# Graph layer and expert layer: first edge runs read at fixed places, adjacency columns in six groups, a third of the weighting on GpSimd, x weighed before it is normalised

## The chip, the core and the metric

The kernel runs on one core of one Trainium2 chip. The metric is device time in microseconds (us), start to end, of one execution. The engines named below are TensorE (PE, with PEld for its weight loads), VectorE (DVE), ScalarE (ACT), GpSimd (POOL) and SyncE (SP, which here only issues DMAs).

## The reference, cut to what matters

```python
# x: 2048 x 256; src, dst: 67584 edges, sorted by dst; edge_weight: one per edge
# node_vec1: 2048 x 1; 8 experts, W1 256 x 1024, W2 1024 x 256
def gnn(xn, values, indices, bias):
    row, col = indices
    return segment_sum(values[:, None] * xn[col], row, 2048) + bias
def ffn(xt, ...):                        # top 2 of 8 experts per token
    top_p, top_idx = top_k(softmax(xt @ Wr + br), 2)
    weights = top_p / top_p.sum(-1)
    xe = layernorm(xt) * ln_g[e] + ln_b[e]
    y = gelu(xe @ W1[e] + b1[e]) @ W2[e] + b2[e]
    return sum over the two experts of weights * y
x = x + gnn(layernorm(x), edge_weight, stack([src, dst]), node_vec1)
x = x + ffn(layernorm(x))
```

All of it is float32. The change touches only the graph layer, and what is prepared beside it.

## The kernel before, in words

**The graph layer as dense products.** The sparse matrix is turned into a dense one of 2048 x 2048, column block by column block, and then multiplied by the normalised x. There are 16 column blocks (`NB`) of 128 nodes. Since `dst` is sorted, the edges of two neighbouring nodes lie in one window of 128 edges. A quarter-like unit `q` (8 of them) covers 128 such pairs of nodes, one on each partition.

- `find_blocks`, `get_run`, `count_before` and `get_win` find where each pair's window starts. The first edge of each of 128 stretches (`first_i`) is spread over the partitions with a small matmul, compared with the nodes' numbers (`less`), and gives a stretch; an indirect DMA from the POOL queue fetches that stretch (`run`, 528 edges), ACT counts the edges before the pair (`sign`), and three more indirect DMAs fetch the window's sources, destinations and weights (`win_s`, `win_d`, `win_w`).
- `keys_of` makes two keys of each edge (source modulo 128; node of the pair and source block), `turn_keys` turns them and the weights with TensorE, and `next_part` splits a weight into three bf16 parts (`w`, three wide) that add up to the float32 value.
- `make_hots(n)` works on a half block, 32 pairs of nodes, of which there are 32. Three DVE instructions (L293, L296, L300): `hl` is one where an edge has a given low key, `eq` one where it has a given high key, and `hr` is `eq` times the three weight parts. All three read two bf16 tensors in SBUF.
- `make_cols(n)` multiplies them: 96 small TensorE matmuls (L320), three parts for each pair; ACT copies the result out (`ar`, L323), a DMA writes it to device memory (`ad`), and after every second half block another DMA reads the whole column block back as `ac` (L327).
- `dense(g, b)` multiplies group `g` of column blocks (`CB` = 4 blocks a group) by `xn_sb`, for two row blocks: 8 products, each of two float32 matmul records (L334). `add` adds the two results into `acc` on DVE (L339).

**The order.** It is written out by hand (`manual_schedule`), engine by engine in the order of the program. A loop over the 32 half blocks makes the hots of `n + 1`, adds what the last half block multiplied, makes the columns of `n`, and from half block 9 on multiplies an older group. Keys and parts of later units, the layer norm's statistics (`block_stats`), the normalising of x (`xn_sb`, L439), its turning and the router's part of it (L446, L456) lie at fixed half blocks. Ten of the 16 blocks' statistics are taken before the loop, six after its first half block. After the loop the last group (blocks 12 to 15) is multiplied beside the router's work (`square`, `roots`, `scales`, `logits`, `best`, `count`, `choose`): 64 products, in eight steps `p` of 8. Then the experts run, the same in both kernels.

**Queues.** SP issues `ad` and `ac` in program order. POOL issues the indirect DMAs in program order; in the loop they come in sets of four (three windows, one run).

Of the kernel before, what the change touches and what calls it, by code (L numbers as in the profile page):

```python
# [22 lines left out]
P = 128  # L23
# [4 lines left out]
def kernel(  # L28
# [45 lines left out]
    CB = 4  # L74
# [19 lines left out]
    first_i = xpool.tile([P, 1], I32, name="first_i")  # L94
    nc.sync.dma_start(first_i, dst.rearrange("(p j) -> p j", p=P)[:, 0:1])

# [3 lines left out]
    for q in range(4):  # L100
        s = slice(q * NB // 4, (q + 1) * NB // 4)
        (nc.sync, nc.scalar)[q % 2].dma_start(acc[:, s, :D], xv[:, s, :])
    nv_rows = small.tile([NB, P], F32, name="nv_rows", bufs=1)
    nc.sync.dma_start(nv_rows, node_vec1.rearrange("(b p) o -> b (p o)", p=P))
    b1_rows = small.tile([NE * KH, P], F32, name="b1_rows", bufs=1)
    nc.sync.dma_start(b1_rows, b1.rearrange("e (c p) -> (e c) p", p=P))
    g_rows = small.tile([NE * KD, P], F32, name="g_rows", bufs=1)
    nc.sync.dma_start(g_rows, ln_g.rearrange("e (k p) -> (e k) p", p=P))
    be_rows = small.tile([NE * KD, P], F32, name="be_rows", bufs=1)
    nc.sync.dma_start(be_rows, ln_b.rearrange("e (k p) -> (e k) p", p=P))  # L110
    wr_sb = consts.tile([P, KD, NE], F32, name="wr_sb")
    nc.scalar.dma_start(wr_sb, Wr.rearrange("(k p) e -> p k e", p=P))
    br_sb = consts.tile([P, NE], F32, name="br_sb")
    nc.scalar.dma_start(br_sb, bass.AP(tensor=br.tensor, offset=br.offset, ap=[[0, P], [1, NE]]))


    ident = consts.tile([P, P], F32, name="ident")
    make_identity(nc, ident)
    jp = consts.tile([P, P], I32, name="jp")
# [3 lines left out]
    ones = consts.tile([P, P], F32, name="ones")  # L123
    nc.vector.memset(ones, 1.0)
    ones_b = consts.tile([P, P], BF16, name="ones_b")
    nc.vector.memset(ones_b, 1.0)
    iota_p = consts.tile([P, P], F32, name="iota_p")
    nc.gpsimd.iota(iota_p, pattern=[[1, P]], base=0, channel_multiplier=0,
                   allow_small_or_imprecise_dtypes=True)
    eps_sb = consts.tile([P, 1], F32, name="eps_sb")  # L130
    nc.vector.memset(eps_sb, EPS)
# [23 lines left out]

    iota_b = consts.tile([P, P], BF16, name="iota_b")
    nc.vector.tensor_copy(iota_b, iota_p)
    iota_h = consts.tile([P, P], F16, name="iota_h")
    nc.vector.tensor_copy(iota_h, iota_p)
    col0 = consts.tile([P, GQ], F32, name="col0")  # L160
    nc.gpsimd.iota(col0, pattern=[[GC * P, GQ]], base=0, channel_multiplier=GC,
                   allow_small_or_imprecise_dtypes=True)
    col16 = consts.tile([P, GQ], F32, name="col16")
    nc.vector.tensor_scalar(col16, col0, -float(NB), None, op0=OP.mult)
    colm = consts.tile([P, GQ], F32, name="colm")
    nc.vector.tensor_scalar(colm, col0, -1.0, -0.5, op0=OP.mult, op1=OP.add)
    colp = consts.tile([P, GQ], F32, name="colp")
    nc.vector.tensor_scalar(colp, col0, 1.0, -0.5, op0=OP.mult, op1=OP.add)
    c15 = consts.tile([P, 1], F32, name="c15")
    nc.vector.memset(c15, 1.5)  # L170

    cols_1 = gnn.enter_context(tc.tile_pool(name="cols_1", bufs=CB))
    ps_s = gnn.enter_context(tc.tile_pool(name="ps_s", bufs=2, space=PSUM))
    edges = gnn.enter_context(ExitStack())
    cols_0 = edges.enter_context(tc.tile_pool(name="cols_0", bufs=CB))
    pool = lambda name, bufs, **k: edges.enter_context(tc.tile_pool(name=name, bufs=bufs, **k))
    find = pool("find", 1)
    one_d = lambda t: t.rearrange("(e o) -> e o", o=1)  # L180
    wins = [None] * GQ
    runs = [None] * GQ
# [3 lines left out]
    mid = find.tile([P, GQ], F32, name="mid")  # L186
# [3 lines left out]
    def find_blocks(pf, q0, q1):  # L190
        less = find.tile([P, GQ, P], F32, name="less")
        l = less[:, q0:q1, :]
        nc.vector.tensor_tensor(l, pf[:, None, :].to_broadcast([P, q1 - q0, P]),
                                col0[:, q0:q1, None].to_broadcast([P, q1 - q0, P]), OP.is_lt)
        nc.vector.tensor_reduce(blk[:, q0:q1], l, AX.X, OP.add)
        nc.vector.tensor_scalar(blk[:, q0:q1], blk[:, q0:q1], -1.0, 0.0, op0=OP.add, op1=OP.max)
        nc.vector.tensor_copy(blk_i[:, q0:q1], blk[:, q0:q1])
        nc.vector.tensor_scalar(mid[:, q0:q1], blk[:, q0:q1], float(EJ), EJ / 2, op0=OP.mult,
                                op1=OP.add)
# [10 lines left out]
    def count_before(q):  # L210
        sign = find.tile([P, EJ], BF16, name="sign")
        nc.scalar.activation(sign, runs[q], AF.Sign, bias=colp[:, q:q + 1], scale=-1.0,
                             accum_out=at[:, q:q + 1])
# [21 lines left out]

# [4 lines left out]
    rowsp = pool("rowsp", 3)  # L240
# [7 lines left out]
    def keys_of(q):  # L248


        s_i, d_i, _ = wins[q]
        cl = prep.tile([P, P], F32, name="cl")
        nc.scalar.activation(cl, d_i, AF.Identity, bias=col16[:, q:q + 1], scale=float(NB))
# [3 lines left out]
        nc.vector.scalar_tensor_tensor(f[:, 0, :], b_i, -float(P), s_i, op0=OP.mult, op1=OP.add)  # L257
        nc.vector.tensor_tensor(f[:, 1, :], cl, b_i, OP.add)
        return f

    def turn_keys(q, f):


        pk = ps_k.tile([P, 3, P], F32, name="pk")
        for i in range(2):
            nc.tensor.transpose(pk[:, i, :], f[:, i, :], ident)  # L266
        nc.tensor.transpose(pk[:, 2, :], wins[q][2], ident)
        w2 = keys.tile([P, P, 3, 2], BF16, name="w2")
        nc.scalar.copy(w2[:, :, 0, :], pk[:, 2, :, None].to_broadcast([P, P, 2]))
        k2 = keys.tile([P, 2, P, 2], BF16, name="k2")  # L270
        for i in range(2):
            nc.scalar.copy(k2[:, i], pk[:, i, :, None].to_broadcast([P, P, 2]))
        parts[q] = (k2, w2, pk[:, 2, :])
# [5 lines left out]
    def next_part(q, i):  # L279

        k2, w2, rest = parts[q]
        r = prep.tile([P, P], F32, name=f"r{i}")
        nc.vector.tensor_tensor(r, rest, w2[:, :, i - 1, 0], OP.subtract)  # L283
        nc.scalar.copy(w2[:, :, i, :], r[:, :, None].to_broadcast([P, P, 2]))
        parts[q] = (k2, w2, r)

    def make_hots(n):


        k2, w2, _ = parts[n // 4]  # L290
        g = n % 4
        hl = hotl.tile([P, GH, P], BF16, name="hl")
        nc.vector.tensor_tensor(hl.rearrange("p g (n t) -> p g n t", t=2),  # L293
                                two(k2[:, 0], g, P), pair(P), OP.is_equal)
        eq = hotr.tile([P, GH, RK], BF16, name="eq")
        nc.vector.tensor_tensor(eq.rearrange("p g (n t) -> p g n t", t=2),  # L296
                                two(k2[:, 1], g, RK), pair(RK), OP.is_equal)
        hr = hotr.tile([P, GH, 3, RK], BF16, name="hr")
# [3 lines left out]
            eq[:, :, None, :].to_broadcast([P, GH, 3, RK]),  # L302
            w[:, :, None, :].to_broadcast([P, GH * 3, RK // 2, 2]), OP.mult)
        return hl, hr

    def make_cols(n, hl, hr):


        cb, h = n // 2, n % 2
        if h == 0:  # L310
            ads[cb] = dram.tile([P, NB, P], F32, name="ad", bufs=CB)
        ad_v = ads[cb].rearrange("(m j) b r -> (j b) m r", m=GB // QP)
        ar = rowsp.tile([P, GH // QP, P], F32, name="ar")
        for m0 in range(0, GH // QP, 4):
            pa = ps_a.tile([P, 4, P], F32, name="pa")
# [28 lines left out]
    with tc.manual_schedule(engines=ALL):  # L344
# [29 lines left out]
        for n in range(NH):  # L374
# [16 lines left out]
            for p in late:  # L391
                add(*p)
# [709 lines left out]
```

## Time and profile before

| What | Value |
|---|---|
| median of 14 runs | 525.72 us (521.97 to 533.76) |
| profiled execution, its own time | 523.11 us |
| its span | 521.3 us |
| busy in the span: PE, DVE, ACT, POOL | 450.0, 282.4, 190.4, 156.0 us |
| busy from 27.69 to 207.03 us (the loop from the second `hl` to the last `hr`): PE, DVE, ACT, POOL | 151.84, 167.00, 74.19, 44.84 us of 179.34 |
| busy from 207.03 to 257.23 us (last group, router): PE, DVE | 48.44, 23.73 us of 50.20 |
| busy from 257.23 us to the end (experts): PE, DVE | 246.63, 74.26 us of 264.07 |

Busy time is what the instructions of an engine cover in a stretch; an engine that covers nearly all of a stretch sets its length there, and one that covers little of it waits or has nothing to do. The three stretches have different limits, so the shares over the whole span say little about any of them.

### The profile page before, as it was taken

The page shows a single profiled execution, that of the slowest core. Times are in us where ns is not written, and L with a number is a line of the kernel's source. Part 1 is how long each engine was busy: PE and PEld are TensorE (multiplying, and loading weights), DVE is VectorE, ACT ScalarE, POOL GpSimd, SP SyncE. Part 2 cuts the span into 40 slices and gives each one's busy share as a digit, 9 for nine tenths or more (in the row PEclk, how much of TensorE's full clock was granted, in tenths as well). Part 3 has the DMA queues.
Part 4 walks back from the last instruction along what each step waited for, and adds up shares of the span by engine and source line. Part 5 has one row for each costly group of instructions (what it writes and reads, how often), then busy time and mean ns, then how long its engine had stood idle before and what let it go on. Part 6 is the DMA issues. An engine that isn't in the chain of part 4 may idle for free. (4 is left out here: it accounts for less than half of the span.)

```text
span 521.3 us, 12093 instructions
## 1 busy us (share of the span) xinstructions
PE 450.0 (86%) x4996; PEld 386.0 (74%) x4996; DVE 282.4 (54%) x594; ACT 190.4 (37%) x438; POOL 156.0 (30%) x127
## 2 busy tenths in 40 slices
PE   0144887999999889899999999999999999997991
PEld 0043786787777678788887888888888888886881
DVE  5698999998999997227848222243323222210011
ACT  1424886432242411037483332323233333322220
POOL 3504044360512000000142444544344334422321
PEclk9986799999999999999999999999999999999997
DMA  6215776776657567795513997799998767748421
GB/s 208 72 42 145 222 233 216 221 238 210 180 176 212 166 175 240 251 347 174 175 53 81 291 334 206 215 353 367 349 335 275 198 175 191 207 108 285 122 105 37
DMA packets 87604, 106.75 MB, mean 205 GB/s; under 512 B 8640, under 2 KB 77360, under 8 KB 85424
## 3 DMA queue, kind: packets, MB, share of 16 engines
q1 hardware_dynamic: 78032, 90.73, 54.4%
q0 software_dynamic: 8032, 14.04, 11.6%
q10 hardware_dynamic: 1472, 1.06, 0.7%
q8 instruction: 44, 0.72, 0.6%
q14 instruction: 24, 0.20, 0.1%
HBM read 79.78 MB, written 28.14 MB: 207 GB/s over the span
## 5 line engine op out<-in xcount | busy, mean ns | idle before, releaser
L919 PE MATMUL ph<-xeT,w 128*128 128x256 f32 (+1 forms) x576 | 123.9, 372 | 5.5 <-PEq L1059 3.9
L334 PE MATMUL py<-xn_sb,ac 128*128 128x264 f32 x512 | 120.9, 391 | 5.0 <-DMA ac<-ad 3.3
L933 PE MATMUL py<-w,hT 128*128 128x256 f32 x544 | 120.6, 379 | 0.0
L919 PEld LDWEIGHTS ph<-xeT,w 128*128 128x128 f32 x576 | 105.1, 192 | 20.3 <-issue 5.3
L921 ACT ACTIVATE hT<-ph,ec 128x256 f32<-128x256 f32 (+1 forms) x144 | 65.9, 461 | 136.9 <-PE ph L919 83.3
L334 PEld LDWEIGHTS py<-xn_sb,ac 128*128 128x128 f32 x512 | 95.0, 190 | 24.3 <-DMA ac<-ad 4.1
L933 PEld LDWEIGHTS py<-w,hT 128*128 128x128 f32 x544 | 102.0, 190 | 13.2
L941 POOL DMA_INDIRECT y_d<-ys,to_i x30 | 48.9, 1631 | 110.1 <-DVE ys L936 90.3
L320 PE MATMUL pa<-hl,hr 128*32 128x128 bf16 x3072 | 55.8, 234 | 20.8 <-DVE hr L300 17.1
L293 DVE TENSOR_TENSOR hl<-k,iota_b 128x4096 bf16<-128x4096 bf16 x32 | 73.1, 2284 | 0.9 <-PE pa L320 0.9
L320 PEld LDWEIGHTS <-hr 128*32 128x32 bf16 x3072 | 49.1, 104 | 29.5 <-DVE hr L300 18.7
L851 POOL DMA_INDIRECT xs<-xr_d,to_i x40 | 41.9, 1047 | 66.9 <-DVE r L617 40.2
L300 DVE TENSOR_TENSOR hr<-eq,w 128x3072 bf16<-128x3072 bf16 x32 | 56.3, 1758 | 2.0 <-DVE eq L296 0.5
L936 DVE SCALAR_TENSOR_TENSOR ys<-py,wt,b2w 128x256 f32<-128x256 f32 x34 | 16.3, 483 | 75.0 <-PE py L933 60.4
L893 DVE TENSOR_SCALAR xeT<-px,ec 128x256 f32<-128x256 f32 (+1 forms) x38 | 18.4, 526 | 63.3 <-PE px L884 56.8
L323 ACT COPY ar<-pa 128x512 f32<-128x512 f32 x64 | 35.6, 585 | 34.1 <-PE pa L320 33.3
L222 POOL DMA_INDIRECT win_s<-in_src,at_i x8 | 11.7, 1456 | 92.4 <-DVE r L283 87.8
L339 DVE TENSOR_TENSOR acc<-acc,py 128x528 f32<-128x528 f32 x32 | 22.1, 698 | 21.5 <-PE py L334 21.5
L908 ACT ACTIVATE b2w<-b,wt 128x256 f32<-128x256 f32 x36 | 16.3, 500 | 27.8 <-DVE wt L906 22.5
L266 PE MATMUL pk<-ident,f 128*128 128x128 f32 x16 | 4.5, 333 | 21.1 <-DVE f L257 16.5
L296 DVE TENSOR_TENSOR eq<-k,iota_b 128x1024 bf16<-128x1024 bf16 x32 | 21.9, 684 | 0.0
L266 PEld LDWEIGHTS pk<-ident,f 128*128 128x128 f32 x16 | 2.3, 153 | 23.3 <-issue 13.3
(193 smaller groups left out, 308.9 us busy)
## 6 DMA issues: line engine op xcount, KB each, us to landing
w<-in_L_ffn_W SPq DMA_DIRECT2D x44, 1024.0 KB, 9.3
ad<-ar SPq DMA_DIRECT2D x32, 512.0 KB, 5.1
ac<-ad SPq DMA_DIRECT2D x16, 1024.0 KB, 5.8
b<-in_L_ffn_b SPq DMA_DIRECT2D x22, 128.0 KB, 9.9
out<-y_d SPq DMA_DIRECT2D x4, 512.0 KB, 6.3
xr_d<-rec SPq DMA_DIRECT2D x1, 1300.0 KB, 6.6
y_d<-acc SPq DMA_DIRECT2D x1, 1280.0 KB, 5.9
acc<-in_x ACTq DMA_DIRECT2D x2, 512.0 KB, 5.5
```

The source lines that it names most:

```text
L293: nc.vector.tensor_tensor(hl.rearrange("p g (n t) -> p g n t", t=2), two(k2[:, 0], g, P), pair(P), OP.is_equal)
L296: nc.vector.tensor_tensor(eq.rearrange("p g (n t) -> p g n t", t=2), two(k2[:, 1], g, RK), pair(RK), OP.is_equal)
L300: nc.vector.tensor_tensor(hr.rearrange("p g i (n t) -> p (g i) n t", t=2), eq[:, :, None, :].to_broadcast([P, GH, 3, RK]), w[:, :, None, : ...
L320: nc.tensor.matmul(pa[j * RK:(j + 1) * RK, m, :], hr[:, g, i, :], hl[:, g, :], start=(i == 0), stop=(i == 2), tile_position=(0, j * RK))
L323: nc.scalar.copy(ar[:, m0:m0 + 4, :], pa)
L334: nc.tensor.matmul(pa[:, i, :DX], acs[g * CB + c][:, b + i, :], xn_sb[:, g * CB + c, :], start=(c == 0), stop=(c == CB - 1))
L339: nc.vector.tensor_add(acc[:, b:b + 2, :], acc[:, b:b + 2, :], pa[:, :, :DX])
L851: nc.gpsimd.indirect_dma_start(out=(sets[s.set][0] if into is None else into)[:, t, :], out_offset=None, in_=(xr_d if rows is None else ro ...
L919: nc.tensor.matmul(ph, w1[:, k, c * P:(c + 1) * P], xeT[:, k, :], start=(k == 0), stop=(k == KD - 1))
L921: nc.scalar.activation(hT[:, c, :s.n * P], ph, AF.Gelu, bias=ec[:, c:c + 1], scale=1.0)
L933: nc.tensor.matmul(py, hT[:, c, t * P:(t + 1) * P], w2[:, c, :], start=(c == 0), stop=(c == KH - 1))
L941: st = nc.gpsimd.indirect_dma_start(out=y_d[:, :], out_offset=bass.IndirectOffsetOnAxis(ap=tos[s.to][:, t:t + 1], axis=0), in_=ys, in_offs ...
```

## The change

In words, by place in the code:

- **Start.** The stretch in which the first unit's windows are looked for (`run_0`, 656 edges a partition) is read by three plain DMAs from fixed places, issued from SP and ACT ahead of x. The first unit needs no search; `find_blocks` is called once for the other seven, with a bf16 `less`, after the first windows are asked for. An activation of the square root stands first on ACT. x is loaded behind `run_0`.
- **Keys.** `keys_of` and `turn_keys` are cut into `low_key`, `high_key`, `turn_key`, `turn_weights` and `count_own`, which are placed one by one.
- **Hots.** `hr` has two weight parts instead of three on DVE. The third part has its own tile (`w3`), and GpSimd multiplies it by `eq` into `hr3`, a tensor_tensor of 128 x 1024 bf16.
- **Columns.** Results are copied out and stored in two halves of 64 partitions' worth of nodes, and each half block is read back by itself (`load_cols`), one half block later.
- **Groups.** Column blocks are multiplied in groups of 2, 2, 3, 3, 3 and 3. In each half block up to `QUOTA` = 8 products are issued, as soon as a group has been complete for `LAG` half blocks. The results are added at the start of the next half block (`do_adds`). The first group's adds also add `node_vec1` (`add_first`), which ACT added before.
- **x.** x is turned and multiplied by the router's weights before it is normalised; a DVE multiplication scales the product (`weighed_x`). Statistics are taken two blocks a half block inside the loop, and normalising goes four blocks at a time.
- Some pools have more buffers: `rowsp` 5 instead of 3, `cols_0` 8 instead of 4, one more `tos`.

```diff
-    CB = 4
+    STEP = E // NG
+    BACK = 4 * STEP
+    RUN_0 = 2 * BACK + P
+    GROUPS = (2, 2, 3, 3, 3, 3)
+    CB0 = 8
+    QUOTA = 8
+    LAG = 3
...
+    nc.scalar.activation(warm_s, eps_sb, AF.Sqrt)
+    run_0 = find.tile([P, RUN_0], I32, name="run_0")
+    nc.sync.dma_start(run_0[16:, :], part(dst, 16 * STEP - BACK, STEP, P - 16, RUN_0))
+    nc.scalar.dma_start(run_0[:nf, :], part(dst, 0, 0, nf, RUN_0))
+    nc.scalar.dma_start(run_0[nf:16, :], part(dst, 0, STEP, 16 - nf, RUN_0))
...
+    def turn_key(q, f, i):
+        nc.tensor.transpose(pk[:, i, :], f[:, i, :], ident)
+        nc.scalar.copy(k2[:, i], pk[:, i, :, None].to_broadcast([P, P, 2]))
...
     def next_part(q, i):
-        nc.scalar.copy(w2[:, :, i, :], r[:, :, None].to_broadcast([P, P, 2]))
+        nc.scalar.copy(w2[:, :, 1, :] if i == 1 else w3, r[:, :, None].to_broadcast([P, P, 2]))
...
-        hr = hotr.tile([P, GH, 3, RK], BF16, name="hr")
+        hr = hotr.tile([P, GH, 2, RK], BF16, name="hr")
         nc.vector.tensor_tensor(
             hr.rearrange("p g i (n t) -> p (g i) n t", t=2),
-            eq[:, :, None, :].to_broadcast([P, GH, 3, RK]),
-            w[:, :, None, :].to_broadcast([P, GH * 3, RK // 2, 2]), OP.mult)
+            eq[:, :, None, :].to_broadcast([P, GH, 2, RK]),
+            w[:, :, None, :].to_broadcast([P, GH * 2, RK // 2, 2]), OP.mult)
+        hr3 = hotr.tile([P, GH, RK], BF16, name="hr3")
+        nc.gpsimd.tensor_tensor(hr3.rearrange("p g (n t) -> p g n t", t=2),
+                                eq.rearrange("p g (n t) -> p g n t", t=2),
+                                two(w3, g, RK), OP.mult)
...
+    def load_cols(n):
+        cb, h = n // 2, n % 2
+        nc.sync.dma_start(acs[cb][h * GH * GC:(h + 1) * GH * GC], ads.pop(n))
...
+    def add_first(b, pa):
+        for i in range(2):
+            nc.vector.scalar_tensor_tensor(acc[:, b + i, :D], pa[:, i, :D], nv_c[:, b + i:b + i + 1],
+                                           acc[:, b + i, :D], op0=OP.add, op1=OP.add)
+        nc.vector.tensor_add(acc[:, b:b + 2, D:], acc[:, b:b + 2, D:], pa[:, :, D:DX])
...
+        count_before(0)
+        get_win(0)
...
+        find_blocks(pf, 1, GQ)
+        get_run(1)
+        get_run(2)
+        get_run(3)
+        xTs = {0: turn_x(0)}
+        b_i, f = low_key(0)
+        turn_key(0, f, 0)
+        block_stats(bn, mv, acc, range(0, 1))
+        high_key(0, b_i, f)
+        turn_key(0, f, 1)
+        hl = make_hl(0)
+        turn_weights(0)
+        next_part(0, 1)
+        eq = make_eq(0)
+        next_part(0, 2)
+        hots = {0: (hl, *make_hr(0, eq))}
...
         for n in range(NH):
+            do_adds()
             if n + 1 < NH:
                 hots[n + 1] = make_hots(n + 1)
...
+            for i in range(2):
+                make_cols(n, i, *hots[n])
+            if n > 0:
+                load_cols(n - 1)
+            while ready < last_g and 2 * group_of[ready][-1] + 1 + LAG - (not jobs) <= n:
+                for b in range(0, NB, 2):
+                    box = []
+                    jobs += [(ready, b + j, c, box) for j in range(2) for c in group_of[ready]]
+                ready += 1
+            more_dense(QUOTA)
...
+            if n < 8:
+                b0 = 4 * (n // 2)
+                if n < 7:
+                    block_stats(bn, mv, acc, range(2 * n + 2, 2 * n + 4))
+                if n % 2 == 0:
+                    weigh_x(b0, xTs.pop(b0))
+                else:
+                    scale_x(b0, 4)
+                    weighed_x(b0, 4)
+                    if b0 + 4 < NB:
+                        xTs[b0 + 4] = turn_x(b0 + 4)
...
-        for p in late:
-            add(*p)
+        load_cols(NH - 1)
+        while jobs:
+            more_dense(2 * max(GROUPS))
+            do_adds()
+        do_adds()
```

In the changed program DVE's order in a half block of the loop is: the adds of the last half block, `hl`, `eq`, `hr`, then that half block's key or part work and statistics. POOL's order is `hr3` of each half block, and every four half blocks the set of three or four indirect DMAs ahead of the next `hr3`.

## The prediction

> **What bounds the kernel now.** I read the page's groups first, then busy time by stretch, then who waits for whom, then DVE and POOL in order of time. The experts' stretch (257 us to the end) is untouched, so all lies in the first 257 us. The costliest groups there, from the page (columns: busy us, mean ns of one, idle time before it and its cause):
>
> ```profile
> L320 PE MATMUL pa<-hl,hr 128*32 128x128 bf16 x3072 | 55.8, 234 | 20.8 <-DVE hr L300 17.1
> L293 DVE TENSOR_TENSOR hl<-k,iota_b 128x4096 bf16<-128x4096 bf16 x32 | 73.1, 2284 | 0.9 <-PE pa L320 0.9
> L300 DVE TENSOR_TENSOR hr<-eq,w 128x3072 bf16<-128x3072 bf16 x32 | 56.3, 1758 | 2.0 <-DVE eq L296 0.5
> L339 DVE TENSOR_TENSOR acc<-acc,py 128x528 f32<-128x528 f32 x32 | 22.1, 698 | 21.5 <-PE py L334 21.5
> ```
>
> The columns' matmuls wait for DVE's `hr`; `hl` hardly ever waits. The stretches (columns: PE, PEld, DVE, ACT, POOL busy) say the same of the loop:
>
> ```profile
> 27.69:207.03 179.34, 151.84 (x3451) 127.76 (x3452) 167.00 (x181) 74.19 (x171) 44.84 (x22) 0.94 0.64 192
> ```
>
> DVE covers 167.0 of 179.3 us, PE 151.8. So DVE sets the loop, and PE would at about 20 us less. Before the loop a chain of transfers sets the time, after it a chain of small DVE and ACT work.
>
> The row that matters most for what is added is how POOL stands to DVE. In order of time (start, duration), DVE and then POOL:
>
> ```profile
> 85.22 2.28 DVE L293 TENSOR_TENSOR hl<-k,iota_b 128x4096 bf16<-128x4096 bf16 x1
> 87.42 0.68 DVE L296 TENSOR_TENSOR eq<-k,iota_b 128x1024 bf16<-128x1024 bf16 x1
> 88.14 1.76 DVE L300 TENSOR_TENSOR hr<-eq,w 128x3072 bf16<-128x3072 bf16 x1
> ```
> ```profile
> 41.76 0.94 POOL L222 DMA_INDIRECT win_s<-in_src,at_i  x1 [18.73 <-DVE r L283]
> ...
> 85.33 2.99 POOL L222 DMA_INDIRECT win_s<-in_src,at_i  x1 [13.15 <-DVE r L283]
> 88.62 2.09 POOL L222 DMA_INDIRECT win_d<-in_dst,at_i  x1 [0.30 <-issue]
> ```
>
> An indirect DMA takes POOL 0.94 us when DVE is free of the three hot instructions. Started under one, it ends 0.82 us after that instruction's end: 88.32 against 87.50 (`hl`), 90.71 against 89.90 (`hr`). POOL, which has indices to read from SBUF, is held for as long as a DVE instruction reads two SBUF tensors, and gets in when it ends. Under the adds (PSUM and SBUF) it is not held: 0.95 us at 107.03.
>
> **The change part by part.** The sum is made against the profiled execution, 523.1 us (span 521.3). That is 2.6 us under the median of the runs, 525.7, and I add 2.6 at the end.
>
> *Start.* Rows before:
>
> ```profile
> 10.55 1.28 ACT L212 ACT_TABLE_LOAD   x1 [10.55 <-DMA run<-in_dst,blk_i]
> 11.85 0.73 ACT L212 ACTIVATE sign<-run,colp 128x528 bf16<-128x528 int32 x1
> ...
> 13.33 0.95 POOL L222 DMA_INDIRECT win_s<-in_src,at_i  x1 [4.27 <-DVE at_i L218]
> ```
>
> `run_0` heads the queues at 0.76 us. A tiny load landed in 2.05 us (`first_i`), a run of nearly this size beside x in 5.0 (5.53 to 10.55). I take 4.0, so 4.8 us. `sign` over 656 instead of 528 elements takes 0.91, its accumulator 0.19, and the two DVE steps and the way to POOL 0.65 as now: the windows are asked for at 6.5 us, not 13.33: -6.8. The table is loaded earlier by the square root (the trace shows `sign` running after that table without a new load). From there to `hl(0)`, at 22.61, it was 9.3 us, with a second unit's keys and two weight parts ahead of it. With only the two keys ahead it is `f` (17.94), turned (0.47) and copied (0.38), 18.9 on the old clock, 5.6 us after the windows: -3.7. From `hl(0)` to `hl(1)` the parts, `eq` and the statistics now lie between: 5.8 instead of 5.1, and 0.8 of POOL's hold: +1.5. Start: **-9.0** (ends: -5, if `run_0` needs the 5.0 us and the windows queue behind x; -11).
>
> *DVE in the loop, POOL left aside.* 1024 elements cost 0.537 us ((1.758 - 0.684) / 2), so `hr` saves 0.537 x 31 = -16.6. Adds: 20 lie in the stretch now; six groups make 48 of them, some 38 in the stretch. 30 plain ones, +10 x 0.65 = +6.5. Eight `add_first`, each two of the 0.483 us kind (L936) and a small one, 1.1: +8.8. Statistics of 14 blocks instead of 6, 0.57 each: +4.6. Four small scalings: +1.5. Together +4.8. DVE's waits for ACT's key copies (2.4 and 1.5 us) and for `cols` (1.6) should go, -5. So **0**: what the smaller `hr` saves is eaten by adds and statistics.
>
> *GpSimd's part.* `hr3` waits for `eq`, is held by `hr`, gets in when `hr` ends, and reads two SBUF tensors. No row shows DVE waiting for POOL. If POOL's reading excludes DVE's as DVE's excludes POOL's, DVE's next two-input instruction waits T, the time of `hr3`. T's bounds come from POOL's rows:
>
> ```profile
> L837 POOL IOTA place<- 128x256 f32 x1 | 0.3, 345 | 2.5 <-DVEq L495 2.5
> masks.py:199 POOL TENSOR_SCALAR_AFFINE_SELECT ident<-ident 128x128 f32<-128x128 f32 x1 | 0.3, 283 | 0.0
> ...
> L128 POOL IOTA iota_p<- 128x128 f32 x1 | 0.2, 233 | 0.0
> ```
>
> Iota, which only writes: 0.875 ns an element, 0.12 us fixed: 1.0 us for 1024, the low end. The select, which reads one and writes one: 1.27 ns, 1.4 us. Two reads at that rate: 2.7 us, the high end. I take 1.4, the only row with a read. Of the 31 stretches from `hr` to the next `hl`, 14 begin with key work or the second part, which read two SBUF tensors, and wait all of T. 17 begin with adds or statistics, which do not, and hide 0.8 on average. 14 x 1.4 + 17 x 0.6 = **+30** (1.0: +18; 2.7: +70; no exclusion: 0).
>
> The Trainium skill's page "SBUF — State Buffer" ("Who interferes with whom") says that a DVE instruction with two SBUF inputs and a GpSimd instruction that reads SBUF exclude each other for the whole instruction, whichever came first. The trace shows it in one direction; the rule speaks against this change, and without the other direction the sum would lose the 30. "GPSIMD Engine Reference" (section 3.1) gives 4497 ns for a two-input add of 2048; half of that is an estimate of 2.25 us, and 14 x 2.25 + 17 x 1.45 = 56 would make the time 569.
>
> *PE.* All 256 products stay. 16 move into the loop, +7.6 us (32 records of 0.239 apart) on 151.8: hidden while DVE takes 179 or more; without that cover PE's floor is 159.5.
>
> *Columns' DMAs.* The same bytes in 64 stores and 32 loads on SP. A load now queues behind the next half block's stores, but a group is used three half blocks after its last column (over 15 us), against 5.1 us for a store and 5.8 for a load: 0. Of the last group it is used 16 products and the branch later (7.4 + 1.4), the same as now: 0 to +1.
>
> *After the loop.* Rows now:
>
> ```profile
> 235.87 0.70 DVE L339 TENSOR_TENSOR acc<-acc,py 128x528 f32<-128x528 f32 x1 [2.86 <-PE py L334]
> ...
> 244.63 2.89 DVE L738 TENSOR_TENSOR chosen<-pos,place 128x1280 f32<-128x1280 f32 x2
> ...
> 247.48 8.80 PE L746 MATMUL px<-chosen,rec 128*128 128x256 f32 x40
> ```
>
> The last group is 48 products, 22.9 us instead of 30.6. But `chosen` ends 11.65 us after the fifth step's add, and that is DVE and ACT work that stays. Up to that add PE does five steps of 6 products instead of 8, 14.4 instead of 18.2. **-3.8**; then the small work is late, and PE waits some 3 us for it. ACT's 16 additions of `node_vec1` (0.5 each) cost nothing now and gain nothing.
>
> Sum: 523.1 - 9.0 + 0 + 30 - 3.8 = 540.3, and 2.6: **543 us**.
>
> **The rivals.**
> - *A: POOL does not hold DVE; faster.* `hr3` lies beside DVE, and only start and end count: 523.1 - 12.8 + 2.6 = 513 (507 if the loop also loses DVE's other waits). For it: in no row is DVE late after a POOL read, `hl` takes 2.28 us each time. Against: those reads are only indices. It decides where DVE loses under 12.8 us, 0.4 us a half block.
> - *B: POOL's queue.* Even so, the sets of indirect DMAs stand ahead of `hr3`. Six sets took 7.4, 8.6, 10.7, 8.8, 8.2 and 6.0 us, mean 8.3, while POOL has some 4.4 us free between two `hr3`: 3.9 x 6 = 23 us of PE waiting, of which DVE, a half block ahead, wins back about half: 513 + 12 = 525, up to 536.
> - *C: columns late.* If SP's split stores and loads take twice the time to land, PE waits at each of five groups some 2 to 3 us, on top of A: 525.
>
> **How the numbers follow.** My case 0.55, A 0.27, B 0.14, C 0.04. My case alone runs from 531 (T of 1.0) to 567 (T of 2.2). The range has to reach A: 507 to 566; above lie T beyond 2.2, below a PE-bound loop. A measurement tells about 0.5% (2.6 us) from no change. Faster: A and a little of B and C, 0.29. Within 0.5%: half of B and C, 0.08. Slower: 0.63.
>
> **What would show it.** Right: a gap of about T ahead of the instruction after `hr` on DVE, `hl` spaced 6.5 to 7 us apart instead of 5.2 to 6, PE waiting in the loop for `hr3`, the first `hl` at about 12 us, `chosen` some 26 us after the last group's first product. Wrong, if DVE's spacing is that of its own durations (A), or PE waits for `hr3` only once in four half blocks, behind the sets (B), or on `ac` (C).

## The result, and the profile after

The changed kernel takes 574.5 us (median of 10 runs, 573.2 to 575.0), the kernel before 525.9 us beside it (47 runs, 520.5 to 534.6): ratio 1.0936, 95% interval 1.0908 to 1.0965. The forecast was 543, with a range of 507 to 566. It had the sign right and the size wrong: the time lies above the range. The experiments were run on three chips, on which the kernel before took 530.9 to 534.5 us in the median. Their ratios leave out runs in a slower state, so they are not the quotients of the medians. Differences in microseconds between two experiments are taken between their own medians; where two experiments ran on different chips, the ratios are the safer comparison.

The profiled execution took 573.3 us, with a span of 571.5, against 523.1 and 521.3 before. The page's groups that answer to those shown of before (busy us, mean ns of one, idle time before it and its cause):

```profile
L336 POOL TENSOR_TENSOR hr<-eq,w 128x1024 bf16<-128x1024 bf16 x32 | 86.9, 2717 | 112.2 <-DVE eq L322 107.3
L358 PE MATMUL pa<-hl,hr 128*32 128x128 bf16 x3072 | 65.1, 249 | 33.8 <-POOL hr L336 27.7
L315 DVE TENSOR_TENSOR hl<-k,iota_b 128x4096 bf16<-128x4096 bf16 x32 | 79.3, 2477 | 0.0
L386 DVE TENSOR_TENSOR acc<-acc,py 128x528 f32<-128x528 f32 x40 | 27.6, 699 | 44.7 <-PE py L374 44.5
L331 DVE TENSOR_TENSOR hr<-eq,w 128x2048 bf16<-128x2048 bf16 x32 | 43.0, 1345 | 1.1
```

`hl` now takes 2477 ns in the mean instead of 2284, though it computes the same. The columns' products now wait mostly for GpSimd's `hr3` (27.7 of 33.8 us; the profile names it `hr`, as it does DVE's), and DVE waits for products ahead of its adds, which in the loop of before it never did. The loop, from the second `hl` to the end of the last `hr` (columns: PE, PEld, DVE, ACT, POOL busy, granted clock, DMA share, GB/s):

```profile
20.82:261.17 240.35, 183.46 (x3463) 148.72 (x3455) 203.35 (x240) 72.53 (x170) 123.15 (x56) 0.86 0.59 146
```

It takes 240.35 us instead of 179.34, and DVE covers 85% of it instead of 93%. So DVE's busy time has grown by 36 us, its idle time by 25. Around the loop little moved. At the start (ACT and POOL in order of time, start and duration):

```profile
4.29 0.84 ACT L231 ACTIVATE sign<-run,colp 128x656 bf16<-128x656 int32 x1 [1.44 <-DMA run<-in_dst]
```
```profile
5.90 1.13 POOL L241 DMA_INDIRECT win_s<-in_src,at_i  x1 [3.30 <-DVE first L477]
```

The first windows are asked for at 5.90 us instead of 13.33, and the first `hl` starts at 14.41 instead of 22.61, the second at 20.82 instead of 27.69. In the tail (DVE, then PE):

```profile
297.80 2.89 DVE L847 TENSOR_TENSOR chosen<-pos,place 128x1280 f32<-128x1280 f32 x2
```
```profile
299.77 1.46 PE L855 MATMUL px<-chosen,rec 128*128 128x256 f32 x6
```

From the last `hr` to the first `px` it is 38.6 us now and was 40.45. Against the prediction's own steps:

| Stretch | predicted | profile after less before |
|---|---|---|
| to the second `hl` | -9.0 | -6.9 |
| loop | 0 + 30 | +61.0 |
| last `hr` to first `px` | -3.8 | -1.9 |
| experts, to the end | 0 | -2.1 |
| sum | +17 | +50 |

All that is wrong lies in the loop. How GpSimd and DVE stand to each other there is seen at 110 us. DVE, and then POOL, in order of time:

```profile
109.25 0.68 DVE L322 TENSOR_TENSOR eq<-k,iota_b 128x1024 bf16<-128x1024 bf16 x1
109.97 1.22 DVE L331 TENSOR_TENSOR hr<-eq,w 128x2048 bf16<-128x2048 bf16 x1
111.11 2.00 DVE L302 TENSOR_TENSOR r<-r,w 128x128 f32<-128x128 f32 x1
```
```profile
110.07 2.88 POOL L336 TENSOR_TENSOR hr<-eq,w 128x1024 bf16<-128x1024 bf16 x1 [4.65 <-DVE eq L322]
```

`hr3` starts when `eq` is done, is held until `hr` ends at 111.19, and ends at 112.95. DVE's `r`, which takes 0.325 us elsewhere, starts at 111.11 and ends at 113.11, right behind it. So GpSimd holds DVE as DVE holds GpSimd. The hold does not show as a gap on DVE, but as an instruction six times its own length. By form, in the loop (DVE):

```profile
L302 DVE TENSOR_TENSOR r<-r,w 128x128 f32<-128x128 f32 x7 | 13.2, 1891 | 0.5 <-ACT w L303 0.5
L271 DVE TENSOR_SCALAR b_i<-win_s 128x128 int32<-128x128 int32 x7 | 11.8, 1688 | 0.0
```

Against their own durations (325 and 220 ns) these two lose 11.0 and 10.3 us, and `hl`, `hr` and `eq` lose 6.2, 3.9 and 3.4: 34.8 us in all. These last three are not held in every half block: `hr` once (5.08 us long, at 28.86), `eq` twice and `hl` six times.

### The profile page after: what moved, and what is told of

It is laid out like the page before. It is cut to its first block, busy times and chain, and to the rows that moved or that the text cites. A ratio compares the mean times of both kernels' runs of the same rounds, so it can differ in the third digit from the quotient of the medians.

```text
span 571.5 us, 12316 instructions
## 1 busy us (share of the span) xinstructions
PE 479.4 (84%) x4996; PEld 404.7 (71%) x4996; DVE 314.0 (55%) x632; ACT 186.6 (33%) x429; POOL 234.2 (41%) x159
## 5 line engine op out<-in xcount | busy, mean ns | idle before, releaser
L374 PE MATMUL py<-xn_sb,ac 128*128 128x264 f32 x512 | 132.8, 417 | 11.5 <-DMA ac<-ad 9.5
L336 POOL TENSOR_TENSOR hr<-eq,w 128x1024 bf16<-128x1024 bf16 x32 | 86.9, 2717 | 112.2 <-DVE eq L322 107.3
L374 PEld LDWEIGHTS py<-xn_sb,ac 128*128 128x128 f32 x512 | 102.5, 206 | 34.6 <-issue 9.1
L358 PE MATMUL pa<-hl,hr 128*32 128x128 bf16 x3072 | 65.1, 249 | 33.8 <-POOL hr L336 27.7
L358 PEld LDWEIGHTS <-hr 128*32 128x32 bf16 x3072 | 54.7, 111 | 45.2 <-POOL hr L336 30.7
L315 DVE TENSOR_TENSOR hl<-k,iota_b 128x4096 bf16<-128x4096 bf16 x32 | 79.3, 2477 | 0.0
L386 DVE TENSOR_TENSOR acc<-acc,py 128x528 f32<-128x528 f32 x40 | 27.6, 699 | 44.7 <-PE py L374 44.5
L331 DVE TENSOR_TENSOR hr<-eq,w 128x2048 bf16<-128x2048 bf16 x32 | 43.0, 1345 | 1.1
L322 DVE TENSOR_TENSOR eq<-k,iota_b 128x1024 bf16<-128x1024 bf16 x32 | 25.3, 790 | 0.0
L303 ACT CAST w<-r 128x256 bf16<-128x256 f32 x16 | 6.5, 405 | 56.6 <-DVE r L302 30.1
```

Source lines behind the costliest of these rows:

```text
L331: nc.vector.tensor_tensor(hr.rearrange("p g i (n t) -> p (g i) n t", t=2), eq[:, :, None, :].to_broadcast([P, GH, 2, RK]), w[:, :, None, : ...
L336: nc.gpsimd.tensor_tensor(hr3.rearrange("p g (n t) -> p g n t", t=2), eq.rearrange("p g (n t) -> p g n t", t=2), two(w3, g, RK), OP.mult)
L358: nc.tensor.matmul(pa[j * RK:(j + 1) * RK, m, :], hr[:, g, k, :] if k < 2 else hr3[:, g, :], hl[:, g, :], start=(k == 0), stop=(k == 2), t ...
L374: nc.tensor.matmul(pa[:, b % 2, :DX], acs[c][:, b, :], xn_sb[:, c, :], start=(c == group_of[g][0]), stop=(c == group_of[g][-1]))
L386: nc.vector.tensor_add(acc[:, b:b + 2, :], acc[:, b:b + 2, :], pa[:, :, :DX])
```

## The experiments

**Theory L**: GpSimd's reading holds DVE, and that is most of the loss. **Rivals**: POOL's queue and the late `hr3` (Q), or the columns (C).

### All three parts on DVE again

```diff
-        hr = hotr.tile([P, GH, 2, RK], BF16, name="hr")
+        hr = hotr.tile([P, GH, 3, RK], BF16, name="hr")
...
-        nc.gpsimd.tensor_tensor(hr3..., eq..., two(w3, g, RK), OP.mult)
```

> The changed kernel with all three weight parts multiplied on DVE again (one hr of 3072 elements); everything else as changed. Theory L (GpSimd's reading of SBUF and a DVE instruction with two SBUF inputs exclude each other, both ways): in the changed kernel's loop the DVE instructions behind hr3 are some 36 us longer than their own durations, and DVE waits 27 us for adds that PE delivers late; hr costs 16.6 us more. So 574.5 - 36 + 16.6 - 10 to 27: 528 to 545 us. Theory C (the loss is in the columns: groups used too early, adds at the start of a half block): the time stays above 555 us.

Measured: 547.7 us (546.0 to 550.2), where before took 531.5; ratio 1.0282 (1.0204 to 1.0361). That is 27 us under the changed kernel, by the ratios 34. In microseconds it is 3 over what L gave, on another chip than the changed kernel's, and it is under the 555 of C. But it is not the kernel before: 2.8% are left over, though its start and tail are the faster ones. Its loop:

```profile
20.38:238.00 217.62, 178.58 (x3451) 145.02 (x3443) 185.15 (x240) 72.24 (x170) 44.53 (x28) 0.89 0.65 163
```

DVE's work is 18 us over that of before (adds, first adds, statistics and scalings, 21.4 by the prediction's terms), and DVE idles 32 us instead of 12.

### The kernel before, with the third part on GpSimd alone

```diff
-        hr = hotr.tile([P, GH, 3, RK], BF16, name="hr")
+        hr = hotr.tile([P, GH, 2, RK], BF16, name="hr")
+        hr3 = hotr.tile([P, GH, RK], BF16, name="hr3")
+        nc.gpsimd.tensor_tensor(hr3..., eq..., two(w3, g, RK), OP.mult)
```

> The kernel before with only the third weight part moved to GpSimd. Theory L: 31 half blocks, of which each loses 1.9 us less what adds hide (0.7 us in 20 of them) and gains 0.54: +25 to +40 us, 551 to 566. Theory Q (GpSimd's queue: hr3 behind the sets of indirect DMAs, PE waits, DVE is not held): +10 to +20 us, 536 to 546. Theory C: within 5 us of before.

Measured: 550.1 us, 18.7 over before; ratio 1.0315 (1.0243 to 1.0387). In microseconds that is 1 under L's bound, and as an increase it lies in Q's range (10 to 20), so the time alone does not decide between them. The trace has L's signature, on instructions that here come first behind `hr` (DVE in the loop):

```profile
L294 DVE TENSOR_TENSOR hl<-k,iota_b 128x4096 bf16<-128x4096 bf16 x31 | 82.1, 2647 | 5.8 <-PE py L462 5.8
L217 DVE SCALAR_TENSOR_TENSOR at<-at,mid 128x1 f32<-128x1 f32 x6 | 11.2, 1868 | 0.0
```

An instruction of one element per partition, 153 ns before, takes 1868. So this part of the change makes the kernel slower by itself, in spite of the 16.6 us that the smaller `hr` saves.

### Reading or being busy: the multiplication unused, and writes alone

Both add unused GpSimd work to the kernel with all parts on DVE. Nobody waits for it.

```diff
+        dm = hotr.tile([P, GH, RK], BF16, name="dm", bufs=1)
+        nc.gpsimd.tensor_tensor(dm..., eq..., two(k2[:, 1], g, RK), OP.mult)
```

> e1 (all parts on DVE) with a GpSimd multiplication of the same size and operands' shapes added in each half block, whose result nobody uses. Leaves nothing out. Theory L: it holds DVE as hr3 did: e1 + 25 to 45 us. Theory Q: nobody waits for it, so e1 + 0 to 5 us.

```diff
+        nc.vector.memset(dm[:, 0:1], 0.0)
+        for _ in range(4):
+            nc.gpsimd.iota(dm, pattern=[[1, 448]], base=0, channel_multiplier=0)
```

> e1 with four GpSimd iotas of 448 elements in each half block (about 2.0 us of GpSimd time, written to SBUF, nothing read) and a one-element DVE memset to pace them (31 x 0.07 us = 2 us). Theory L: writing does not hold DVE: e1 + 2 to 5 us. If any GpSimd work beside DVE costs time: e1 + 20 us or more.

Measured: 585.2 us with the multiplication (ratio 1.0977, 1.0902 to 1.1052), 549.7 with the writes (1.0325, 1.0241 to 1.041), against 547.7 without either, on the same chip: +37.5 and +1.9. Of the multiplication, and then of the writes (DVE in the loop):

```profile
L271 DVE TENSOR_SCALAR b_i<-win_s 128x128 int32<-128x128 int32 x7 | 13.5, 1933 | 0.0
L302 DVE TENSOR_TENSOR r<-r,w 128x128 f32<-128x128 f32 x7 | 13.5, 1924 | 0.5 <-ACT w L303 0.5
```
```profile
L315 DVE TENSOR_TENSOR hl<-k,iota_b 128x4096 bf16<-128x4096 bf16 x31 | 70.7, 2282 | 0.0
```

The writes kept POOL busy for 62.9 us in 124 instructions, and `hl` took its own 2282 ns. So GpSimd being busy does not hold DVE, and a GpSimd instruction that reads does: no wait for `hr3` and no queue is needed for it. L stands, Q is not needed. The Trainium skill's page "SBUF — State Buffer" ("Who interferes with whom") has both halves of this: a GpSimd instruction that only writes does not contend with a two-input DVE instruction, one that reads does, and the first to come keeps the other out to its end.

### What is left: the order of adds, and of the columns' loads

Two rows of the kernel with all parts on DVE pointed at waits. PE waited 9.5 us for columns, where a group of 3 began with nothing left of the group before; and DVE waited 20.2 us for products ahead of plain adds in the loop (25.1 with the first ones behind it), which the change had put ahead of the hot instructions. Who waited for whom in its loop (us, times, longest):

```profile
DVE acc L382 <- PE py L370: 20.2, 8, 8.4
PE py L370 <- DMA ac<-ad: 9.5, 3, 4.9
```

```diff
-            do_adds()
             if n + 1 < NH:
                 hots[n + 1] = make_hots(n + 1)
+            do_adds()
```

> The kernel with all three parts on DVE (547.7 us where before took 531.5, +16.2), with one step changed: a half block's adds stand behind the hot instructions of the next half block on DVE instead of ahead of them, as in before. In that run DVE waited 25.1 us for products ahead of plain adds, 2.2 ahead of first adds, and its loop took 217.6 us for 185.2 us of DVE work. Theory O (adds at the head tie DVE to PE: what PE is late by stops the hot instructions too, and then PE for want of them): the waits ahead of adds fall under 8 us and the time falls by 12 to 20 us, to a ratio of 0.99 to 1.01. Theory S (the columns that come late at two group starts are the cause, 9.5 us of PE waiting): the time falls by 0 to 5 us, ratio 1.02 to 1.03, and PE still waits some 9 us for the columns.

```diff
-            if n > 0:
-                load_cols(n - 1)
+            load_cols(n)
```

> The kernel with all three parts on DVE, with one step changed: each half block's columns are read back right behind their own stores, not one half block later. Theory S: PE's waits for the columns (9.5 us) and DVE's two long waits behind them (8.4 us each at the starts of groups 2 and 4) go, and the time falls by 8 to 16 us, ratio 0.998 to 1.013. Theory O: DVE still waits some 10 us ahead of adds outside of those starts; the time falls by 2 to 8 us, ratio 1.013 to 1.025.

> Both steps together: adds behind the hot instructions, and columns read back at once. If both hold DVE, the loop comes near DVE's own 185 us plus some 5 us, 22 to 27 us under the kernel with all parts on DVE: ratio 0.977 to 0.988. If either alone accounts for it all, no more than 16 to 20 us, ratio 0.99 to 1.0. If PE (178.6 us busy in that loop, at a granted clock of 0.89) is the bound, 10 to 14 us, ratio 1.0 to 1.01.

The fourth of this set undoes two more steps besides:

```diff
-    adds_due.append(partial(add if g else add_first, b - 1, box[0]))
+    adds_due.append(partial(add, b - 1, box[0]))
...
                     weighed_x(b0, 4)
+                    for b in range(b0, b0 + 4):
+                        nc.scalar.activation(acc[:, b, :D], acc[:, b, :D], AF.Identity, bias=nv_c[:, b:b + 1])
...
+        block_stats(bn, mv, acc, range(0, 4))
         b_i, f = low_key(0)
```

> The last with two steps of the change undone besides: ACT adds node_vec1 (16 instructions of some 0.5 us) and all adds are the plain kind, and the statistics of four blocks are taken before the first keys, while DVE waits for windows. That takes 8.3 - 5.6 = 2.7 us and 2 to 4 x 0.57 = 1.1 to 2.3 us from DVE's loop. If DVE sets the loop: 3 to 5 us under the last kernel, ratio 0.968 to 0.982. If PE does: the same within 1 us.

Measured, on one chip: 548.8, 554.2, 553.2 and 556.6 us (ratios 1.0373, 1.0487, 1.0462 and 1.0526, intervals of 0.006 to 0.008 to each side). The kernel that they change ran on another chip, at a ratio of 1.0282; by the ratios not one got faster, and both theories missed. The first run's waits (from the second `hl` to the experts):

```profile
DVE acc L382 <- PE py L370: 26.3, 11, 4.2
DVE hl L315 <- PE pa L354: 8.3, 5, 5.7
PE py L370 <- DVE acc L382: 7.5, 7, 4.1
PE py L370 <- DMA ac<-ad: 4.4, 2, 3.7
```

Its loop became 7.3 us shorter (210.3), its tail 7.2 longer: the first `px` starts at 273.7 us in both. Of DVE's 26.3 us, 22.7 lie behind the loop. In the loop DVE now waits for PE to be done with older columns (8.3 us), and PE's products for adds (7.5 us, 3.4 of them in the loop), which in the kernel with the adds ahead they did not. The program suggests the reason: the products go into two buffers, each for two row blocks, which in groups of 3 is 6 products, while a half block issues 8. A half block so fills one buffer and a part of the next, and PE is out of buffers until DVE adds. So in groups of 3 late adds hold PE, where early ones hold DVE; this is argued from the program and these waits, not shown by a run of its own. The loads at once did not take the wait for columns away: PE waited 9.0 us for them in the second run, 9.5 without that step. Why the loads at once cost 4.4 us (third run against first), and less DVE work another 3.4 (fourth against third), stays open.

### Groups, and TensorE's clock

**Theory K**: the kernel with all parts on DVE issues products where the granted clock is low (0.50 from 46 us on; 0.77 and 0.66 behind half blocks 13 and 14, where no group was ready), so PE is slower there. **Theory D**: it is DVE's added work.

K misread its first row. At 46 us PE multiplies columns; the first dense product starts at 61.1 us (81.7 in before), and up to 70 us these took 394 ns, against 391 in the mean of before. Its second row holds: behind half blocks 13 and 14, 26 of these matmul records took 483 ns in the mean (136 to 146 us). Three runs, on one chip:

```diff
-    GROUPS = (2, 2, 3, 3, 3, 3)
-    CB0 = 8
+    GROUPS = (4, 4, 4, 4)
+    CB0 = 4
...
-            acs[cb] = (cols_1 if cb in group_of[last_g] else cols_0).tile(...)
+            acs[cb] = (cols_1 if cb // 4 % 2 else cols_0).tile(...)
```

> The kernel with all three parts on DVE (547.7 us, ratio 1.028 to before), with one thing changed: column blocks in groups of 4, 4, 4, 4, so that the first products are issued at half block 9 and products are there in every half block from then on, as in before. The two orders tried were not the cause. Theory K (TensorE's clock: in that kernel products were issued from 46 us on, where the granted clock was 0.50, and again around half blocks 13 and 14, where no group was ready, PE stood half idle and the clock fell to 0.77 and 0.66; in before they begin at about 73 us at 1.00 and there is no such gap): dense products fall from 408 ns to 395 or less, the clock of the loop rises from 0.89 to 0.93 or more, and the time falls by 14 to 24 us, 11 of them for 16 fewer adds on DVE: ratio 0.983 to 1.002. Theory D (DVE's added work is the cause: adds, first adds, statistics, scalings, 18 us in the loop): 7 to 11 us, ratio 1.007 to 1.015, and DVE covers nearly all of the loop. If it is in neither (columns in halves, x weighed raw): within 5 us, ratio over 1.018.

```diff
-            while ready < last_g and 2 * group_of[ready][-1] + 1 + LAG - (not jobs) <= n:
+            while n >= 9 and ready < last_g and 2 * group_of[ready][-1] + 1 + LAG - (not jobs) <= n:
```

> The kernel with all three parts on DVE and its groups of 2, 2, 3, 3, 3, 3, but no product ahead of half block 9. From there on there is no half block without products, and DVE's work is the same, add for add. 24 products are left over after the loop instead of 8, 16 x 2 x 0.239 = 7.6 us. Theory K: dense products at 395 ns or less, the loop (to the last hot instruction) 15 to 22 us shorter, the time 6 to 14 us lower in spite of the 7.6: ratio 1.0 to 1.017. Theory D: the loop no shorter than by those 7.6, the time the same within 4 us: ratio 1.02 to 1.036.

```diff
+            if not jobs and n < 16:
+                idle = ps_s.tile([P, 2, 512], F32, name="py1")
+                for _ in range(12):
+                    nc.tensor.matmul(idle[:, 0, :P], ident, iota_p, start=True, stop=True)
             more_dense(QUOTA)
```

> The kernel with all three parts on DVE, and 12 TensorE products of 128 x 128 float32 that nobody uses (0.27 us each, 3.3 us) in each of the half blocks below 16 that have no products of their own (0 to 4, 13 and 14). This adds work to PE and takes none away. Theory K: the clock stays up, dense products at 398 ns or less, the time 3 to 12 us lower: ratio 1.005 to 1.022. Theory D, or a bound by PE's work itself: the same or up to 15 us more: ratio 1.028 to 1.056.

Measured: 537.9 us with groups of four (ratio 1.0081, 1.003 to 1.0131), 540.6 with products from half block 9 (1.0141, 1.0105 to 1.0176), 547.9 with idle products (1.0199, 1.0124 to 1.0274). Loop of the last, where PE was kept busy:

```profile
21.10:239.30 218.20, 188.20 (x3619) 155.19 (x3611) 185.07 (x240) 72.07 (x170) 44.50 (x28) 0.94 0.65 161
```

The clock of the loop rose from 0.89 to 0.94, and the loop took 218.2 us where it took 217.6; the dense products stayed at 408 ns. Two stretches of it, for PE alone (busy, granted clock, DMA share, GB/s):

```profile
44.00:56.00 12.00, 10.03 (x195) 1.00 1.00 255
128.00:140.00 12.00, 5.63 (x15) 0.61 0.94 218
```

Without the idle products the clock was 0.50 and 0.66 in these two. In the first it is now full, and the tenth `hl` starts at 83.5 us instead of 83.0: nothing waited for the low clock of the early half blocks, and there K falls. Behind half blocks 13 and 14 the idle products ended at 125.9 us, before PE's wait for columns, and did not keep the clock up. There K is not tested. (By its ratio this run lies in K's span; its median is that of the kernel without idle products, but on another chip.) Products from half block 9 made the loop 12.3 us shorter, of which 7.6 were only moved behind it; groups of four 17.5:

```profile
20.60:220.70 200.10, 163.49 (x3419) 130.99 (x3411) 175.63 (x224) 71.33 (x170) 45.98 (x25) 0.90 0.70 175
```

9.5 of the 17.5 are DVE work (185.15 to 175.63, 16 adds fewer), 8 are waits. The ratio of groups of four falls where D had it; the dense products, at 391 ns, fall as K had it, but the clock of the loop, 0.90, does not rise to K's 0.93. Products from half block 9 lie between the two, in K's ratio but with a loop less shortened and dense products at 404 ns.

PE's wait for columns went from 9.5 to 1.1 us in groups of four. How the 8 us divide between that wait and the low clock behind it stays open. 24 us of DVE's idle time are still there, 16.7 of them ahead of adds:

```profile
DVE acc L386 <- PE py L370: 8.4, 4, 4.8
DVE acc L382 <- PE py L370: 8.3, 6, 2.1
```

With one buffer to a half block (4 columns by 2 row blocks are 8 products) these adds could now go behind the hot instructions.

### Groups of four, with the adds behind the hot instructions

The edits of the two shown above together.

> The kernel with all three parts on DVE and groups of four (ratio 1.008), with the adds behind the hot instructions of the next half block. In groups of two and three that step did not help (1.037), but there PE was late by the columns and by the clock. If the adds' place is what is left (30 us of DVE waiting for products): 8 to 15 us lower, ratio 0.98 to 0.993, DVE's waits for products under 10 us in the loop. If PE's own pace is what is left: within 3 us, ratio 1.002 to 1.014, the waits on another line.

Measured: 522.3 us (521.2 to 523.1), where before took 534.5 and groups of four with adds ahead 537.9 on the same chip: ratio 0.9823 (0.9767 to 0.9878). The same edit that did nothing in groups of 2 and 3 gives 15.6 us here. The loop:

```profile
20.60:207.30 186.70, 161.93 (x3422) 133.13 (x3411) 174.86 (x225) 71.92 (x170) 57.35 (x25) 0.87 0.75 188
```

DVE covers 94% of it, about as in before (93%), and waits 0.2 us for products in the loop. The granted clock, 0.87, is under that of the three slower kernels (0.89, 0.90 and 0.94). On this chip this kernel is faster than the kernel before. The profiled execution of before, on record with the prediction, took 523.1 us, so by the two profiles alone they are level. It keeps the change's start, its columns in halves and its handling of x, and leaves out its groups, its adds' place and its GpSimd part.

### The changed kernel with groups of four, its GpSimd part kept

> The changed kernel, its GpSimd part and all, with groups of four alone. If the GpSimd part and the groups cost on their own: the part's 25 to 37 us stay, and the groups' 2% go: 30 us over the kernel with groups of four on DVE, ratio 1.055 to 1.075. If the groups only cost because the GpSimd part makes all late (or the reverse): under 1.05, or still over 1.08.

Measured: 559.5 us (557.7 to 564.3), ratio 1.0553 (1.047 to 1.0635): 15 us under the changed kernel, 21.6 over the kernel with groups of four and all parts on DVE. So each of the two losses is there without the other. Of the GpSimd part (PE's waits, from the second `hl` on; us, times, longest):

```profile
PE pa L358 <- POOL hr L336: 28.3, 17, 5.0
```

### The start alone

```diff
+        count_before(0)
+        get_win(0)
         first = find.tile([P, 1], F32, name="first")
...
-        find_blocks(pf, 0, 1)
-        get_run(0)
...
-        turn_keys(1, f1)
         hots = {0: make_hots(0)}
+        get_win(1)
```

Into the kernel before; the second unit's keys and parts go one half block later each.

> The kernel before with the start of the change alone: the first unit's stretch read at fixed places, the first windows asked for ahead of the search, the first hots ahead of the second unit's keys; groups of 4, adds, x, columns and all three parts on DVE as before. The hot instructions begin 5 to 8 us earlier, and if the loop is what it was, so does all behind them: 4 to 8 us faster, ratio 0.985 to 0.993. If the second unit's keys, now inside the loop, take it back, or the loop waits for TensorE's clock, within 3 us: ratio 0.994 to 1.006.

This missed its aim. The small loads still stood on ACT's queue, ACT came to `sign` behind issuing them only at 12.09 us, and the first `hl` started at 23.75, later than before. Its time, 536.1 us (ratio 0.9984, 0.9938 to 1.0031), says nothing of the start. With the loads moved to SyncE:

> The kernel before with the start of the change alone, now with the small loads behind x on SyncE as the change has them, so that ACT is free to count by some 5 us. The first windows are asked for at 6 us instead of 13.3, the first hot instruction starts at about 16 us instead of 22.6, the second at about 22 instead of 27.7. If the loop is what it was: 4 to 7 us faster, ratio 0.986 to 0.993. If the time is given back in the first half blocks, where the second unit's keys and the statistics now lie and TensorE's clock is at 0.5 to 0.8: within 2.5 us, ratio 0.995 to 1.005.

Measured: 535.8 us, ratio 0.9944 (0.9871 to 1.0017). DVE, in order of time:

```profile
16.88 2.28 DVE L313 TENSOR_TENSOR hl<-k,iota_b 128x4096 bf16<-128x4096 bf16 x1
...
22.62 2.26 DVE L313 TENSOR_TENSOR hl<-k,iota_b 128x4096 bf16<-128x4096 bf16 x1
```

The hot instructions began 5 us earlier. The interval reaches from a gain of 7 us to a loss of 1, so whether the start pays alone stays open. (The profiled execution, 536.9 us, is no guide to where the lead goes: others of this kernel took down to 525.4.) In the kernel with groups of four and adds behind, the ninth `hl` is at 69.0 and the last `hr` ends at 207.3, against 69.1 and 207.0: its 7 us of lead are gone by the ninth half block, where 14 of the 16 blocks' statistics, the first key work and the scalings now lie.

## Why the prediction was wrong

- **Start, -9.0: -6.9.** The windows were asked for 7.4 us earlier (6.8 predicted), and `sign` took 0.84 (0.91). What was mis-sized is the way from there. `win_s` took 6.4 us to land, beside x, and had taken 3.1 before; so the first `hl` came at 14.4 and not at 12. The end "the windows queue behind x" was named for it.
- **GpSimd's part, +30: some 39 in the loop.** The mechanism was right, and shown by itself (+37.5 us for reading, +1.9 for writing); the term was 9 too small. T was taken as 1.4 us, from a row with one read; `hr3` takes 1.9 once it is let in. The 14 half blocks with key work or parts lost 1.52 us each (21.3 / 14; in 12 of them the loss was about 1.7) and the hot instructions 13.5 together, 34.8 where 30 was predicted. DVE's busy time says the same: 203.35 - (185.15 - 16.6) = 34.8. In the profiles the loop with the part is 22.7 us longer than without it, and it saves 16.6 of `hr`: 39.3. The rest, 4.5, is more idle time of DVE; that it comes from PE's 26 us of waiting for `hr3` is likely, but not shown. The Trainium skill's page "GPSIMD Engine Reference" (section 3.1) led to an estimate of 2.25 us for `hr3`; the shortest of 32 took 1.91, so the page's figure was nearer than the row chosen, and measured is still less.
- **DVE in the loop, 0: the step that failed, +21.7.** 217.6 us with all parts on DVE, less 179.3, less the 16.6 that `hr` then doesn't save. The terms of DVE's own work were about right: 18 us more were measured, and 16.6 + 4.8 = 21.4 predicted. What the sum left out is waiting: it took 5 us of DVE's waits away, and DVE's idle time rose from 12.3 to 32.5 us. It costed `do_adds` by its duration, 0.65 us a pair, and its new place at nothing. But at the head of a half block it stands between PE's products and the next hot instructions, and PE cannot begin the next columns without those: neither engine can run ahead. In groups of four that place cost 13.4 us of loop (200.1 to 186.7), and DVE's waits ahead of adds fell with it from 16.7 to 0.2. Groups of two and three cost 17.5, of which 9.5 are adds. This is the split in the order in which the two were undone: the place alone, in groups of two and three, gave nothing.
- **Columns' DMAs, 0.** "A group is used three half blocks after its last column" was wrong for every group that finds no products left: the `- (not jobs)` takes one half block off. In the changed kernel PE waited 9.5 us at two such starts, and DVE 8.0 and 6.8 behind it. That the load now goes out one half block later is not what does it, since with the loads at once 9.0 us stayed. It was a rival (C), with 4% and as an addition to a fast case; it is part of the 17.5.
- **PE hidden, "while DVE takes 179 or more".** True of PE's total, and not the question: PE's 8 products are not hidden where DVE waits for those of each half block.
- **After the loop, -3.8: -1.9**, with GpSimd's part; -4.7 without it (273.7 - 238.0 = 35.7).
- **Rivals.** A (no hold) fell by the traces and by +37.5. B (POOL's queue) is not needed: an unused multiplication, for which nobody waits, costs as much.
- **What would show it.** PE does wait for `hr3`, `chosen` comes 24 us after the last group's first product (some 26 given), and `hl` is spaced 7.9 us apart, where 6.5 to 7 were given. The gap ahead of the instruction after `hr` is not there, because a held instruction is shown as started.

## What to carry to other kernels

Where one engine's step is moved ahead of its producers' next input, ask whom it ties together: an add costs 0.7 us, and the adds' place cost 13 in groups of four. A change of order and a change of sizes belong together (8 products a half block, 6 to a buffer), and one of them measured alone can read as nothing, as the adds' place did. Work that was moved to GpSimd and reads SBUF was not free beside DVE instructions with two inputs in SBUF: a saving of 0.54 us a half block was paid with 1.1 us of held instructions (34.8 / 31).

## What the runs showed of the hardware

- A DVE `tensor_scalar` of one SBUF input (`b_i`, 128 x 128 int32) was held by GpSimd like those with two: 1688 ns instead of 220. The Trainium skill's page "SBUF — State Buffer" ("Who interferes with whom") says that such forms can take the shared ports as well. One with an input in PSUM was not: `r<-pk,w` took 0.28 us at 103.57, inside `hr3`'s 102.54 to 105.43, and the adds kept their 0.70.
- A held instruction is recorded as busy. DVE's busy time in the loop of the changed kernel, 203.35 us, holds 34.8 us of standing still.
- With idle products added, the loop's granted clock was higher (0.94 against 0.89) and its length the same (218.2 against 217.6 us); the kernel of 522.3 us ran its loop at 0.87. The mean clock of these loops does not order their times.
- The kernel before spread from 524.9 to 542.6 us on one chip, the best kernel here from 521.2 to 523.1. Why was not found out.
